# Attention and mixture of experts in one kernel: rows sent a tile earlier, VectorE's work regrouped, three shared blocks and paired row scatters between attention and experts

## The chip, the core and the metric

The kernel runs on one core of a Trainium2 chip. The metric is device time in microseconds (us), the median of several runs. The core's engines each take their instructions in order: PE (TensorE, matmuls), DVE (VectorE), ACT (ScalarE), POOL (GpSimd) and SP (SyncE, here for issuing transfers). They wait for each other through semaphores; transfers run on DMA engines. The xr and ys of the text are buffers in the device's memory.

## The reference

`x` has 4096 rows (tokens) of 256 numbers. Two sublayers are added to it in turn.

- Cross attention: `x = x + LayerNorm(q + Attention(q, ctx) Wo)` with `q = layernorm(x)`, 16 heads of 64, and 77 context rows for each of 4 batches. Per token and head there are 77 scores, a softmax, and a weighted sum of values.
- Mixture of experts: with `h = layernorm(x)`, each token's scores `softmax(h Wg)` over 32 experts pick its best 4. Each of these computes `silu(h W1[e]) * (h W3[e]) @ W2[e]` (256 to 128 to 256) times the score. An expert holds at most 4 x 4096 x 4 / 32 = 2048 pairs. Every token also passes a shared SwiGLU with inner width 256. Both are added to `x`.

All data are 32 bit floats. The 16384 pairs of token and expert must be sorted by expert before the experts' products can be made.

## The kernel before, in words

The 4096 rows are 32 tiles of 128 (`t`), four to a block (`blk`, 0 to 7; `c` is the tile in its block). The code calls block 6 `y` and block 7 `z`.

Attention is folded: prepared products `mq` hold keys times query weights, so that scores come straight from the normalised rows (`scores`, L418), in three groups of 6, 5 and 5 heads. For each group VectorE takes the maxima (L438), ScalarE the exponentials with their sums (`soften`, L441); then VectorE inverts the sums (`invert`, L454), POOL divides (`divide`, L458), PE transposes the probabilities (`turn_p`, L468), and multiplies them with values times output weights (`output`, L491). `residual` (L502) adds the rows. One tile of the loop issues the scores of tile t and the transposes and output of tile t-1.

Around that, the same loop carries the rest of each block in steps at fixed tiles. `measure_in`, `scale_in`, `norm_in`, `turn_in` and `bias_in` prepare the next block; `keep` (L400) adds a bias row to its rows. `measure_out` and `settle` (L508, L517) do the LayerNorm behind the attention, a tile each; `measure_ffn` and `norm_ffn` the one ahead of the experts. Two blocks behind come the experts' scores: `turn_ffn` (transposes pxn, L552), `gate` (lg, L566), `turn_gate`, `chances` and `powers` (softmax), `choose` (the best four, L596), `mark` (one-hot `oh` and `mask`, L619 and L626), `count` (prefix counts by matmul, pf, L638) and `place` (row numbers, L643). `send` (L669) then scatters one row of 128 pairs: POOL issues an indirect DMA which writes 128 rows of 1088 bytes from SBUF to their places in xr. There are 16 of them per block, 128 in all. From tile 11 on the loop sends four per tile, after the division.

When the loop has ended, blocks y and z still have to be sorted. This stretch is called the gap. In it stand, interleaved by hand: the rest of y's and z's steps, the shared SwiGLU of blocks y, 0 and z (`shared_in`, L696, product ph and activation sg; `shared_mid`, L716; `shared_out`, L724, product pz; `shared_add`, L739), and the tables. `tables` (L876) works out from the counts per expert which expert and which rows of xr each of the experts' tiles has: table "a" for tiles 0 to 63, which rest on blocks 0 to 5 alone, in four steps, and table "z" for the others. VectorE copies a table from PSUM at L938 to L941. The gap's scatters are issued in lots, `sends(3)`, `sends(2)`, `sends(7)`, `sends(12)` and `sends(20)`, with no wait between the scatters of a lot; the five transfers of expert weights (`load_experts`, L166) are issued first on SP, 3 MB in all.

The experts follow: 128 tiles of 128 rows in a fixed loop and 16 more in a second one. SP fetches eight tiles at a time (`fetch`, L1030), register loads giving the addresses; each is 136 KB. A tile goes through four steps, one per turn of the loop: transposes pgT (L1089), products peh with the tile's weights (L1097), ScalarE's activation h (L1105), and output py (L1118), which POOL scatters into ys (L1123). At the end every token's four results are gathered and added.

No scheduler moves this work. Inside `as_written` (L327), instructions of an engine keep the order in which the code issues them; only the row scatters that stand in an unbroken run on POOL, and likewise the results, may change places among themselves:

```python
kind = kinds.get(i.name)
before, run, of = runs.get(i.engine, ([], [], None))
if kind is None or kind != of:
    before, run = run, []
for name in before:
    tc.add_manual_dep(i, name, NOSYNC, reason="as written")
```

Of the kernel before, what the change touches and what calls it, by code (L numbers as in the profile page):

```python
# [9 lines left out]
F32 = mybir.dt.float32  # L10
# [20 lines left out]
def kernel(  # L31
# [73 lines left out]
    iota_j = const.tile([P, NJ], F32, name="iota_j")  # L105
    nc.gpsimd.iota(iota_j, [[1, NJ]], base=0, channel_multiplier=0, allow_small_or_imprecise_dtypes=True)
# [260 lines left out]
    def means(name):  # L367
        return sm.tile([P, NC, 2], F32, tag="mv", name=f"mv_{name}", bufs=6)
# [300 lines left out]
    def send(blk, i0, i1):  # L669

        row, xn = rows[blk], xns[blk]
        for i in range(i0, i1):
# [12 lines left out]
            if blk < BA:  # L685
                early.append(sct.ins)
            else:

                tc.declare_no_dep(sct.ins, group="firsts", reason="distinct rows")
                tc.add_to_no_dep_group("lates", sct.ins)  # L690

# [56 lines left out]
    measure_in(0)  # L748
    scale_in(0)
    norm_in(0)  # L750
    turn_in(0)
    bias_in(0)
    keep(0, 0, NC)
    xts[1] = load(1)
    with as_written():
        for t in range(NT):
            blk, c = t // NC, t % NC
            ffn, old = blk - 1, blk - 2
            ahead = blk + 1 < NB
            if c == 0 and blk + 2 < NB:  # L760
                xts[blk + 2] = load(blk + 2)
            if t == 0:

                nc.sync.dma_start(xr[NE * PLACES :, :], none)
                nc.sync.dma_start(
                    xr[: NE * PLACES, :].rearrange("(e q) r -> q e r", q=PLACES)[:P],
                    none.unsqueeze(1).to_broadcast([P, NE, ROW]),
                )
            if t == 18:
                nc.sync.dma_start(ws13[:, :, 0, :], Ws1.rearrange("(k p) f -> p k f", p=P))  # L770
                nc.sync.dma_start(ws13[:, :, 1, :], Ws3.rearrange("(k p) f -> p k f", p=P))
                nc.sync.dma_start(ws2, Ws2.rearrange("(k p) f -> p k f", p=P))
            if t in parts:
                load_experts(*parts[t])
            if c == 1 and ahead:
                scale_in(blk + 1)
            if c == 1 and ffn >= 0:
                measure_out(ffn, 2, 4)
            if c == 3 and ahead:
                bias_in(blk + 1)  # L780
            if c == 3:
                measure_out(blk, 0, 2)
            if c == 3 and ffn >= 0:
                measure_ffn(ffn)
            if c == 1 and old >= 0:
                gate(old)
            if c == 3 and old >= 0:
                count(old)
            sv = [scores(t, g) for g in range(2)]
            if c == 1 and old >= 0:  # L790
                turn_gate(old)
                chances(old)
            soften(t, 0, sv[0])
            if c == 1 and old >= 0:
                powers(old)
            soften(t, 1, sv[1])
            sv.append(scores(t, 2))
            if t >= 1:
                for i in range(3):
                    turn_p(t - 1, i)  # L800
            soften(t, 2, sv[2])
            if c == 0 and old >= 0:
                turn_ffn(old)
            if c == 2 and ahead:
                turn_in(blk + 1)
            if c == 0 and ahead:
                measure_in(blk + 1)
            if c == 1 and old >= 0:
                choose(old)
            if c == 2 and old >= 0:  # L810
                mark(old)
            if c == 3 and old >= 0:
                place(old)
            invert(t)
            divide(t)
            if c == 1 and ahead:
                norm_in(blk + 1)
            if c == 3 and ffn >= 0:
                norm_ffn(ffn)
            if c == 3:  # L820
                settle(blk, 0)
            elif ffn >= 0:
                settle(ffn, c + 1)
            if c >= 2 and ahead:
                keep(blk + 1, 2 * c - 4, 2 * c - 2)
            if t >= 11:
                b11, c11 = divmod(t - 11, NC)
                send(b11, c11 * TOPK, (c11 + 1) * TOPK)
            if t >= 1:
                residual(t - 1, output(t - 1))  # L830

        sxs[0] = late.tile([P, NC, D], F32, tag="qb", name="sx_0", bufs=3)
        sxs[0] = sxs[0].rearrange("p c d -> p (c d)").rearrange("p (k t) -> p k t", k=KC)
        nc.sync.dma_start(sxs[0], xnd[0])
        z, y = NB - 1, NB - 2
        assert BA == y
        msum_a = sm.tile([P, NE], F32, tag="msum_a", name="msum_a", bufs=1)
        nc.vector.tensor_copy(msum_a, cums[BA][:, 0, :])  # L840
        left = [(y - 1, i) for i in range(NK)]

        def sends(n):
            for blk, i in left[:n]:
                send(blk, i, i + 1)
            del left[:n]

# [5 lines left out]
        for i in range(3):  # L853
            turn_p(NT - 1, i)
# [465 lines left out]
```

## Time and profile before

| | us |
|---|---|
| median of three runs (lowest, highest) | 794.02 (792.67, 794.72) |
| time of the profiled execution | 795.5 |
| its span, first to last instruction | 793.7 |
| preparation | 0 to 61.8 |
| attention loop, 32 tiles, about 42.4 a block | 61.8 to 401.6 |
| gap | 401.6 to 482.6 |
| experts | 482.6 to 731 |
| gather, addition and store | 731 to 793.7 |

The mean TensorE clock granted over the span is 0.973. Stretches are cut by hand where one kind of work gives way to the next; the experts' first tiles overlap the end of the gap. To read the profile: an engine's idle time in front of an instruction is put down to the engine whose signal came last. Where no instruction is found whose end fits the signal, the trace names it "remote", or "another core or an unknown queue". Ends of matmuls are modelled. A run of equal instructions may be drawn as one line with a count.

### The profile page before, as it was taken

What the parts mean: (1) busy time and instruction counts of PE and PEld (TensorE: products, weight loads), DVE (VectorE), ACT (ScalarE), POOL (GpSimd) and SP (SyncE); (2) the same over time, 40 slices, a digit from 0 to 9 for tenths busy, and PEclk for the clock granted to TensorE, in tenths of its full rate; (3) what the DMA queues carried; (4) which work ended last, traced back from release to release, by engine and by line L of the source; (5) the groups of instructions that cost most, each with busy time, mean ns of one, the idle gap of its engine ahead of it and who ended that gap; (6) DMA issues with size and microseconds to landing.
All of it is one profiled execution on the core that took longest, in us unless ns stands there. A gap on an engine that the chain in (4) does not pass through costs nothing.

```text
span 793.7 us, 12911 instructions
## 1 busy us (share of the span) xinstructions
PE 726.8 (92%) x3508; PEld 540.2 (68%) x3508; DVE 526.8 (66%) x1455; ACT 334.3 (42%) x1586; POOL 403.3 (51%) x488
## 2 busy tenths in 40 slices
PE   6999999999999999999975569999999999999883
PEld 4775777677777777776743347888888878776452
DVE  1874565787778777776753336666667666564797
ACT  0647666766667776766621002222222222221100
POOL 2003333346878777786887354555555555534000
PEclk9999999999999999999999688999999999999997
DMA  8930000403226131514183523465655544522997
GB/s 270 331 107 1 1 0 2 124 10 114 79 72 213 58 130 57 155 51 142 57 243 107 159 94 110 143 209 178 210 159 170 166 158 143 175 89 74 404 396 282
DMA packets 78866, 111.96 MB, mean 141 GB/s; under 512 B 9995, under 2 KB 63679, under 8 KB 78783
## 3 DMA queue, kind: packets, MB, share of 16 engines
q1 hardware_dynamic: 59663, 66.66, 27.0%
q0 software_dynamic: 13056, 36.72, 12.8%
q10 hardware_dynamic: 6064, 7.64, 2.8%
q8 instruction: 31, 0.51, 0.3%
q14 instruction: 52, 0.43, 0.2%
HBM read 62.36 MB, written 48.64 MB: 140 GB/s over the span
## 4 chain that ended last, share of the span: by engine, by line
PE 66%; DVE 12%; ACT 6%; DMA 4%; another core or an unknown queue 4%; POOL 3%; issue 3%; SPq 0%; DVEq 0%; ACTq 0%; POOLq 0%
PE peh L1097 15%; PE po L497 14%; PE sc L430 13%; PE py L1118 7%; ACT p L446 5%; PE pgT L1089 4%; PE pp L479 2%; DVE gy L1213 2%; PE phT L1111 2%; PE ph L704 2%; DMA gy<-ys 2%; DVE y L1214 1%; POOL xr L674 1%; PE pvo L262 1%
## 5 line engine op out<-in xcount | busy, mean ns | idle before, releaser
L1123 POOL DMA_INDIRECT ys<-y,place x144 | 138.5, 962 | 120.7 <-DVE y L1122 81.0
L446 ACT ACTIVATE p<-sc,mx 128x77 f32<-128x77 f32 x512 | 159.5, 352 | 93.1 <-DVE mx L438 93.1
L1097 PE MATMUL peh<-we,gT 128*128 x576 | 151.9, 387 | 7.6 <-DVE gT L1091 7.1
L497 PE MATMUL po<-we,pT 128*128 128x256 f32 (+1 forms) x640 | 147.4, 384 | 4.6 <-DVE pT L484 3.3
L674 POOL DMA_INDIRECT xr<-xn,row x128 | 127.8, 999 | 46.5 <-issue 35.1
L461 POOL TENSOR_TENSOR p<-p,su 128x385 f32<-128x385 f32 (+1 forms) x96 | 91.1, 974 | 97.4 <-DVE su L456 76.5
L430 PE MATMUL sc<-we,qT 128*128 128x385 f32 (+1 forms) x384 | 138.9, 509 | 0.9 <-POOL qT L416 0.9
L497 PEld LDWEIGHTS po<-we,pT 128*128 128x128 f32 (+1 forms) x640 | 118.4, 190 | 27.1 <-DVE pT L484 5.4
L1105 ACT ACTIVATE h<-peh 128x128 f32<-128x128 f32 x144 | 40.0, 278 | 196.6 <-PE peh L1097 118.8
L446 ACT ACTIVATION_READ_ACCUMULATOR p<-sc,mx 128x1 f32 x512 | 119.4, 233 | 0.0
L1097 PEld LDWEIGHTS peh<-we,gT 128*128 128x128 f32 x576 | 99.9, 193 | 17.2 <-DVE gT L1091 8.4
L430 PEld LDWEIGHTS sc<-we,qT 128*128 128x128 f32 x384 | 71.1, 189 | 54.3 <-issue 27.6
L1106 DVE TENSOR_TENSOR h<-peh,h 128x128 f32<-128x128 f32 x144 | 42.0, 291 | 73.8 <-ACT h L1105 68.7
L1118 PE MATMUL py<-we,ehT 128*128 x288 | 86.6, 383 | 0.0
L1122 DVE TENSOR_SCALAR y<-py,own 128x256 f32<-128x256 f32 x144 | 69.6, 483 | 11.3 <-PE py L1118 10.3
L438 DVE TENSOR_REDUCE mx<-sc 128x5 f32<-128x385 f32 (+1 forms) x96 | 54.3, 576 | 33.2 <-PE sc L430 31.6
L1091 DVE COPY gT<-pgT 128x256 f32<-128x256 f32 x144 | 59.8, 415 | 6.7 <-PE pgT L1089 3.1
L1089 PE MATMUL pgT<-ident,g 128*128 128x128 f32 x288 | 55.6, 276 | 0.4 <-issue 0.4
L1118 PEld LDWEIGHTS py<-we,ehT 128*128 128x128 f32 x288 | 44.0, 193 | 11.9 <-issue 1.2
L1089 PEld LDWEIGHTS pgT<-ident,g 128*128 128x128 f32 x288 | 40.5, 143 | 15.1 <-issue 1.4
L730 PE MATMUL pz<-ws,hT 128*128 128x256 f32 x128 | 34.3, 419 | 15.3 <-DVE hT L719 14.4
L479 PEld LDWEIGHTS pp<-ident,p 128*128 128x128 f32 x320 | 36.1, 138 | 11.4 <-issue 5.5
(200 smaller groups left out, 933.6 us busy)
## 6 DMA issues: line engine op xcount, KB each, us to landing
g<-xr SPq DMA_DIRECT2D x144, 136.0 KB
gy<-ys SPq DMA_DIRECT2D x16, 1024.0 KB
xr<-y SPq DMA_DIRECT2D x1, 4352.0 KB
y<-in_x SPq DMA_DIRECT2D x8, 512.0 KB
out<-y ACTq DMA_DIRECT2D x16, 256.0 KB
xnd<-xnT SPq DMA_DIRECT2D x6, 512.0 KB
we<-in_W SPq DMA_DIRECT2D x8, 384.0 KB
ys<-y,place POOLq DMA_INDIRECT x144
```

The costliest lines, as they stand in the source:

```text
L430: nc.tensor.matmul(sc[:, : (h1 - h0) * SK], qTs[blk][:, k, o : o + P], mq[:, b, k, h0 * SK : h1 * SK], start=(k == 0), stop=(k == KC - 1),)
L438: nc.vector.tensor_reduce(mx[:, h0:h1], sv, AX.X, ALU.max, negate=True)
L446: nc.scalar.activation(probs[t][:, h, :], sv[:, h - h0, :], AF.Exp, bias=mx[:, h : h + 1], accum_out=su[:, h : h + 1],)
L461: nc.gpsimd.tensor_tensor(p[:, h0:h1, :], p[:, h0:h1, :], su[:, h0:h1].unsqueeze(2).to_broadcast([P, h1 - h0, SK]), ALU.mult,)
L497: nc.tensor.matmul(po[:, :D], pT[:n, i, :], vo[b][:n, i, :], start=(i == 0), stop=(i == KT - 1))
L674: sct = nc.gpsimd.indirect_dma_start(out=xr, out_offset=bass.IndirectOffsetOnAxis(ap=row[:, i : i + 1], axis=0), in_=xn[:, c, :], in_offse ...
L1089: nc.tensor.transpose(pt[:, k * P : (k + 1) * P], g[:, j % RG, k * P : (k + 1) * P], ident)
L1091: nc.vector.tensor_copy(gT.rearrange("p k t -> p (k t)"), pt[:, :D])
L1097: nc.tensor.matmul(ph[:, : 2 * H], gT[:, k, :], we[:, ds(ev[j] * EW + k * 2 * H, 2 * H)], start=(k == 0), stop=(k == KC - 1),)
L1118: nc.tensor.matmul(py[:, :D], hT, we[:, ds(ev[j] * EW + KC * 2 * H, D)], start=True, stop=True)
L1122: nc.vector.tensor_scalar(y, py[:, :D], own[:, i, 1:2], None, ALU.mult)
L1123: sent = nc.gpsimd.indirect_dma_start(out=ys, out_offset=bass.IndirectOffsetOnAxis(ap=place_[:, i : i + 1], axis=0), in_=y, in_offset=None,)
```

## The change

The loop: `mark` moves from tile c = 2 to c = 1, behind the division; `count` and `place` from c = 3 to c = 2; so that the sends begin at tile 10, four a tile and six at tile 31, from a list `left`. `keep` of a block moves from the block before (c = 2 and 3, two each) to its own c = 0, ahead of the reciprocal; the first block's `keep` moves from the preparation to tile 0. `settle` of the block before moves: tile 1 ahead of the reciprocal of c = 0, tile 2 behind its division, tile 3 ahead of the reciprocal of c = 2. `measure_in` moves from c = 0 to the c = 3 before it, and `measure_out` is split in halves for c = 0 and c = 1. In the last block, tiles 30 and 31, the normalisation, transposes and gate product of y are issued inside the loop, and the steps of table "a" too, whose wide temporaries share the buffer of `oh`; its expert numbers come from a product with `ones` in place of the helper column `e_col`.

The gap: the same three shared blocks, y, 0 and z. `sends` can make the first scatter of a lot wait for the last instruction issued. y's 16 scatters go out in eight lots of two, the first lot without such a wait; of z's 16, eight go out in the gap in twos and eight in the experts' loop, one every sixth tile. The fetches of the first sixteen experts' tiles are issued in the gap, on SP ahead of the five weight transfers, into a pool of their own.

The built order on POOL behind `place(y)`, where scatters may change places: seven scatters that wait for no such instruction, then one that waits for ScalarE's normalisation of z, two free ones, one that waits for z's transposed copy, and five that wait one after another for PE's pz of y, ScalarE's `powers`, its sg of block 0, VectorE's `shared_mid` and the copy of z's counts. Behind `place(z)`: two free ones, one waiting for sg of z, three free ones, and then one each for pz of block 0, the second sg of z, and pz of z.

The diff, with parts of the tables, of the old gap and of unchanged lines left out:

```diff
+            room = lt2.tile([P, NK, NE], F32, tag="oh", name="room").rearrange("p n e -> p (n e)")
+            oj, t1, t2, t3 = (room[:NE, i * NA : (i + 1) * NA] for i in range(4))
...
-    keep(0, 0, NC)
...
+    z, y = NB - 1, NB - 2
+    assert BA == y
+    left = []
+    def sends(n, after=None):
+        for i, (blk, k) in enumerate(left[:n]):
+            sct = send(blk, k, k + 1)
+            if after is not None and i == 0:
+                tc.add_manual_dep(sct, after, SYNC, reason="rows in small lots")
+        del left[:n]
+    def last():
+        return nc.cur_bb.bb.instructions[-1].name
...
-            if c == 1 and ffn >= 0:
-                measure_out(ffn, 2, 4)
+            if c < 2 and ffn >= 0:
+                measure_out(ffn, 2 + c, 3 + c)
             if c == 3 and ahead:
                 bias_in(blk + 1)
             if c == 3:
                 measure_out(blk, 0, 2)
-            if c == 3 and ffn >= 0:
+            if c == 3 and ffn >= 0 and not end:
...
-            if c == 3 and old >= 0:
-                count(old)
...
+            if c == 2 and old >= 0:
+                count(old)
...
+            if c == 3 and end:
+                turn_ffn(y)
...
+            if c == 3 and end:
+                gate(y)
+                next(ta)
...
-            if c == 0 and ahead:
-                measure_in(blk + 1)
+            if c == 0:
+                keep(blk, 0, NC)
+                if ffn >= 0:
+                    settle(ffn, 1)
             if c == 1 and old >= 0:
                 choose(old)
             if c == 2 and old >= 0:
-                mark(old)
-            if c == 3 and old >= 0:
                 place(old)
+                left += [(old, i) for i in range(NK)]
+            if c == 2 and ffn >= 0:
+                settle(ffn, 3)
+            if c == 3 and blk + 2 < NB:
+                measure_in(blk + 2)
+            if t == 0:
+                measure_in(1)
+            if c == 3 and end:
+                settle(z, 0)
+                next(ta)
...
+            if c == 0 and ffn >= 0:
+                settle(ffn, 2)
...
-            if c == 3 and ffn >= 0:
+            if c == 1 and old >= 0:
+                mark(old)
+            if c == 2 and end:
+                measure_ffn(y)
+            if c == 3 - end and ffn >= 0:
                 norm_ffn(ffn)
-            if c == 3:
+            if c == 3 and not end:
                 settle(blk, 0)
-            elif ffn >= 0:
-                settle(ffn, c + 1)
-            if c >= 2 and ahead:
-                keep(blk + 1, 2 * c - 4, 2 * c - 2)
-            if t >= 11:
-                b11, c11 = divmod(t - 11, NC)
-                send(b11, c11 * TOPK, (c11 + 1) * TOPK)
+            sends(6 if t == NT - 1 else TOPK)
             if t >= 1:
                 residual(t - 1, output(t - 1))
+            if t == NT - 2:
+                ta = tables("a", cums[BA][:, 0, :], NA)
+                next(ta)
...
+        turn_gate(y)
+        next(ta)
+        chances(y)
+        powers(y)
         for i in range(3):
             turn_p(NT - 1, i)
-        settle(z, 2)
-        residual(NT - 1, output(NT - 1))
+        sends(3)
+        choose(y)
+        settle(z, 1)
+        mark(y)
+        po = output(NT - 1)
+        count(y)
+        sends(3, last())
+        assert not left
+        residual(NT - 1, po)
         measure_out(z, 3, 4)
-        gate(y)
-        turn_gate(y)
-        chances(y)
-        powers(y)
-        settle(z, 3)
-        sends(2)
-        measure_ffn(z)
+        place(y)
+        left += [(y, i) for i in range(NK)]
...
+    with as_written():
+        shared_in(y, 0, AF.Tanh)
+        settle(z, 2)
+        settle(z, 3)
+        measure_ffn(z)
+        sends(2)
+        shared_in(y, 1, AF.Tanh)
+        shared_mid(y, 0)
+        norm_ffn(z)
+        sends(2, last())
+        fetch(0)
+        fetch(RG)
+        for part in range(5):
+            load_experts(*parts[NT + 1 + part])
+        shared_mid(y, 1)
+        turn_ffn(z)
+        sends(2, last())
+        shared_out(y)
+        sends(2, last())
+        gate(z)
+        turn_gate(z)
+        chances(z)
+        powers(z)
+        sends(2, last())
+        shared_in(0, 0, AF.Silu)
+        sends(2, last())
+        choose(z)
+        mark(z)
+        shared_mid(0, 0)
+        sends(2, last())
+        shared_in(0, 1, AF.Silu)
+        count(z)
+        msum_z = sm.tile([P, NE], F32, tag="msum_z", name="msum_z", bufs=1)
+        nc.vector.tensor_copy(msum_z, cums[NB][:, 0, :])
+        tz = tables("z", msum_z, NJ - NA)
+        sends(2, last())
+        place(z)
+        assert not left
+        left += [(z, i) for i in range(NK)]
+        shared_mid(0, 1)
+        shared_in(z, 0, AF.Silu)
+        sends(2, last())
+        shared_out(0)
+        sends(2, last())
+        shared_mid(z, 0)
+        shared_add(y)
+        shared_in(z, 1, AF.Silu)
+        sends(2, last())
+        shared_mid(z, 1)
+        shared_add(0)
+        shared_out(z)
+        sends(2, last())
+        shared_add(z)
...
-        fetch(0)
         for j in range(NM_ + len(steps)):
-            if j % RG == 1 and j + RG - 1 <= NM_:
+            if j % RG == 1 and RG < j + RG - 1 <= NM_:
...
+            if j % 6 == 0:
+                sends(1)
```

## The prediction

> **What bounds the kernel now.** I read the page's busy shares and forty slices first, to find where TensorE rests.
>
> ```profile
> PE 726.8 (92%) x3508; PEld 540.2 (68%) x3508; DVE 526.8 (66%) x1455; ACT 334.3 (42%) x1586; POOL 403.3 (51%) x488
> PE   6999999999999999999975569999999999999883
> POOL 2003333346878777786887354555555555534000
> PEclk9999999999999999999999688999999999999997
> ```
>
> PE is the bound except in the slices from about 400 to 480 us, where the clock falls too. The windows cut there (start:end, length, then busy us of PE, PEld, DVE, ACT and POOL, then clock, DMA share, GB/s):
>
> ```profile
> 186.00:228.00 42.00, 41.69 (x205) 30.63 (x203) 32.63 (x90) 29.27 (x154) 32.53 (x41) 1.00 0.29 97
> 401.60:445.70 44.10, 23.01 (x104) 11.66 (x103) 19.00 (x81) 7.79 (x15) 30.69 (x38) 0.85 0.50 161
> 462.80:482.60 19.80, 12.95 (x46) 9.04 (x43) 6.28 (x24) 2.23 (x9) 8.42 (x9) 0.74 0.17 63
> 482.60:580.00 97.40, 95.91 (x532) 80.36 (x532) 67.98 (x220) 24.76 (x115) 55.38 (x59) 1.00 0.55 176
> ```
>
> A block of four attention tiles leaves PE 0.3 us idle, the experts 1.5 in 97. The gap wastes 21 + 7. The chain of waits says on what (start, us, what):
>
> ```profile
> 425.50 17.95 another core or an unknown queue
> 444.62 1.03 DVE mask L626
> 445.69 1.48 PE pf L638 x4
> ...
> 457.80 15.71 another core or an unknown queue
> ```
>
> The timelines show what stood there (start, us, instruction, idle before it):
>
> ```profile
> 425.04 0.27 PE L934 MATMUL p_r_a<-t_a,ones 32*1 32x64 f32 x2
> 443.43 0.21 DVE L938 TENSOR_SCALAR r_tab_a<-p_r_a 1x64 int32<-1x64 f32 x1 [17.93 <-remote]
> 445.69 0.79 PE L638 MATMUL pf<-mask,tri 128*128 128x128 f32 x2 [16.40 <-DVE mask L626]
> 473.53 0.28 ACT L1105 ACTIVATE h<-peh 128x128 f32<-128x128 f32 x1 [15.73 <-remote]
> 410.23 1.57 POOL L674 DMA_INDIRECT xr<-xn,row  x1 [0.19 <-issue]
> 439.43 0.96 POOL L674 DMA_INDIRECT xr<-xn,row  x1 [0.30 <-issue]
> 470.60 0.96 POOL L674 DMA_INDIRECT xr<-xn,row  x1 [0.31 <-issue]
> ```
>
> VectorE's table copy L938 needs only PE's product p_r_a, done at 425.3, yet starts at 443.43. The trace's record of PE's signals has none between 422.10 and 443.40, and then four in 0.16 us. Likewise h (L1105) starts at 473.53, long after peh. Both releases come about 3 us after POOL's last row scatter of an unbroken run: 24 scatters at 1.27 us from 410.23 to 440.4, 15 from 452.85 to 471.6. Signals of the first run begin to lag after four scatters (2.1 us at 414.3), of the second after eight. Loop tiles issue four and show no hold; expert results 1.63 us apart show none. So I read: while scatters run back to back, PE's signals are held. The trace doesn't show by what.
>
> **The change, part by part.** T counts from the scores of tile 31 (382.97 before). Before: the last output ends at T 18.7, experts begin at 79.9 (462.86). Their tiles, 1.63 us apart, count back to a start of 93.6, as 476.6 is tile 9's 491.23 less 9 periods: first matmul at T 83.3, then slow ramp, half clock and 1.7 us for the late gathers of tile 8.
>
> *Loop.* Marking, counting, placing and sending one tile earlier, measure_out in halves, keep and settle at new places: same instructions. PE has 0.3 us of idle per block, so the gain is 0 (at most 7 x 0.3 = 2). Their cover is the stretch to the next reciprocal: after the tile's maxima VectorE waits 4.2 us for the exponentials. With c = 0 it now gets four keeps (4 x 0.43 to 0.68) and settle 1 (0.43 + 0.48 to 1.06) plus half a measure_out (0.6): 3.2 to 4.8. An overrun of 0.6 first eats the 3 us between divide and transposes; if that cover were gone, 0.6 x 7 = 4. I take 0. POOL has 32.5 busy of 42 in a block and sends as many rows per tile, so its queue is no fuller. Only tile 0 shows a late reciprocal: keep(0) leaves the preparation and joins measure_in(1) there. It ended 68.9 and the reciprocal ran at 69.34; 4 x 0.43 more make it 70.6: +1.3, in full, since nothing stands behind.
>
> [...] In the rows settle's last step takes 0.48 alone and 1.06 under a divide, so moving two settles and four keeps off the divides saves VectorE 2 x 0.58 + 4 x 0.25 = 2.2 us per block. [...]
>
> *Tiles 30 and 31.* Gate of block y (6) and table a move in. PE then waits for the normalised block (about 1.6) and its gate chain (1.6), less half a microsecond of the waits that stand there now; output 31 ends near T 21.4 instead of 18.7. In return the gate's product and three of four table steps are over by then.
>
> *The gap.* PE was busy 56.6 of the 79.9 us from the scores of 31 to the experts; 2.1 of it is the low clock of the third window (0.88 of 17.2), so its work is 54.5 at full clock. To it come the 3.2 above. Added: prefix counts of y wait for its mask, 2.7 (chances, powers, choose, mark: from T 15 to 24); the transposes of z wait for its norm, 3.5 without a hold. 54.5 + 3.2 + 2.7 + 3.5 = 63.9. From the first transposes to the first peh it was 3.4 before; I take 4 with its ramp: start 67.9. Removed: the hold on the table, since L938's product is now made in tiles 30 and 31, behind which are no more than six scatters.
>
> *Scatters in twos.* As many as before. The first of a pair waits for the instruction last written, but row scatters may move among themselves and the built order on POOL uses it: after place(y) seven stand in a row without such a wait, then waits come one by one with up to four free ones between. Queued behind each wait are the other scatters and VectorE's place of z through POOL's copies; fetches on SP wait for the landed rows. Bounds: no hold at all, 0; both holds in full, 16.4 + 15.7. [...] By the rows, seven in a row (9 us) are more than the four after which lag began, and less than 24. I take 6 us on y's run and 3 to 5 on z's, 10 in all, with ramp.
>
> *Fetches and weights.* Sixteen gathers (0.53 us each) now stand on SP ahead of five weight loads. First gather when the earlier rows have landed, T 34; sixteen issued by 45, weights by 51. They took 14 us to land before, so T 57 to 65; first use 65 to 74. Hidden, margin near zero at worst. Gathers of tile 8 come early: 1.7 saved. Eight scatters of z go into the experts, one per six tiles: 9 of POOL's idle 40% there; hidden.
>
> *Sum.* Start before 93.6. After, 67.9 + 10 = 77.9, plus 1.3 for tile 0 and 2 for a remaining dip of the clock: 81.2. Gain 12.4. Against the profiled execution, whose span is 793.7 and its whole time 795.5, 783.1; that execution stood 1.5 above the median of the runs, 794.0, so 781.6. I say 782.
>
> **Rivals.** *A, likeliest, 0.42:* holds shrink but remain, 782, own range 776 to 790. *B, holds gone, 0.19:* for it, loop scatters in fours and spaced results show none; against it, the seven in a row. 93.6 - 67.9 - 1.3 = 24.4; with a dip, 795.5 - 24.4 + 2 - 1.5 = 772. *C, the gain is used up, 0.12:* the change doesn't do what it says, because the free scatters run as one train again and one hold of 15 stays on the path: 67.9 + 15.7 + 1.3 + 5 of clock and late weights = 89.9; 795.5 - 3.7 - 1.5 = 790, or, with the loop's overrun of 4, 794. *D, slower, 0.27:* both holds return in full, one on POOL's train behind place(y), one behind place(z), and now stall residual, z's mask and the ramp: 67.9 + 16.4 + 15.7 + 1.3 = 101.3, 7.7 beyond 93.6: 802. It decides once the holds on the path pass 93.6 - 69.2 = 24.4 us. For it: 24 of the 32 scatters of y and z are still in the gap, and seven free ones follow y's place; against it: the waits break the train, and the table's copy no longer lies under it.
>
> **How the numbers follow.** About 0.3%, 2.4 us, is what a measurement of this kernel can tell from no change. A gives 0.39 faster and 0.03 within; B 0.19 faster; C 0.04 faster, 0.06 within, 0.02 slower; D 0.02 within, 0.25 slower: faster 0.62, within 0.11, slower 0.27. The range leaves out one in ten at each end: from half of B's mass, 769, to most of D's, 802.
>
> **What would show it.** Right: no stretch without a PE signal over 6 us; table a's copy within 1 us of its product; first expert transposes near T 74; weights landed before the first peh; loop blocks at 42.0 to 42.5; tile 0's reciprocal at 70.6. Wrong: "remote" waits of 15 us after place(y) or place(z); a peh waiting for its weights; PE idle over 1 us a block before the transposes.

## The result

The changed kernel takes 800.34 us (median of 7, 797.56 to 804.14) beside 794.02 of the kernel before (792.67 to 795.5): ratio 1.0084, 95% interval 1.0059 to 1.0109. It is slower by 0.6% to 1.1%. The profiled execution has a span of 798.6 us, 4.9 more than before.

The page of the changed kernel:

```profile
PE 733.0 (92%) x3508; PEld 541.3 (68%) x3508; DVE 524.1 (66%) x1457; ACT 334.3 (42%) x1586; POOL 401.8 (50%) x501
PE   6998999999999999999994898998999999999883
POOL 2003343357777778777667355656555555534000
PEclk9999999999999999999997799999999999999997
```

PE's hole around 420 us is smaller than before, but two of the four slices between 480 and 560 us have fallen from nines to eights. The windows, cut at the new borders (start:end, length, busy us of PE, PEld, DVE, ACT, POOL, then clock, DMA share, GB/s):

```profile
186.00:228.00 42.00, 41.04 (x202) 30.17 (x201) 31.71 (x88) 29.57 (x154) 31.87 (x42) 1.00 0.29 94
387.40:412.90 25.50, 22.92 (x107) 16.24 (x107) 16.46 (x64) 10.20 (x46) 16.48 (x20) 0.87 0.15 50
412.90:467.20 54.30, 38.75 (x129) 22.25 (x129) 20.97 (x59) 8.68 (x15) 32.95 (x43) 0.84 0.56 176
481.40:588.10 106.70, 97.43 (x514) 77.41 (x513) 65.99 (x214) 24.96 (x112) 60.29 (x63) 1.00 0.53 168
```

A stretch of the loop now has 0.96 us of PE idle, which was 0.31. Tile 31 takes 25.4 us from its scores to its output, which was 18.7, and its granted clock is 0.87. The gap behind it has 15.6 us of idle, and the tiles 8 to 64 of the experts 9.3 in 106.7.

Laid over each other by the starts of the same matmuls, the two traces give a ledger whose parts add up to the spans. The experts' first tiles overlap the gap, so the start of steady experts is reckoned back from tile 8: its first product, less eight periods of 1.627 us. "Start" below always means this, counted from the scores of tile 31.

| stretch | before | after | difference |
|---|---|---|---|
| to the scores of tile 31 | 382.97 | 387.43 | +4.46 |
| from there to the start of steady experts | 91.96 | 81.00 | -10.96 |
| the eight periods | 13.02 | 13.02 | 0 |
| experts, tiles 8 to 64 | 94.26 | 106.69 | +12.43 |
| tile 64 to the end | 211.47 | 210.42 | -1.05 |
| sum | 793.68 | 798.56 | +4.88 |

So the gap did become shorter, by about what was forecast. What it won was lost again by the experts, and the loop's loss came on top.

The chain of waits of the changed kernel shows the remote waits that are left (start, us, what):

```profile
429.59 13.05 another core or an unknown queue
...
514.81 4.09 another core or an unknown queue
...
542.05 4.11 another core or an unknown queue
```

There is one of 13 us in the gap, and new ones of 4 us stand where experts run. Timelines from there, of POOL and of ScalarE:

```profile
511.71 0.96 POOL L1154 DMA_INDIRECT ys<-y,place  x1 [1.96 <-DVE y L1153]
512.97 0.96 POOL L1154 DMA_INDIRECT ys<-y,place  x1 [0.30 <-DVE gT L1122]
514.29 0.96 POOL L1154 DMA_INDIRECT ys<-y,place  x1 [0.36 <-issue]
515.55 0.96 POOL L672 DMA_INDIRECT xr<-xn,row  x1 [0.30 <-issue]
516.81 0.96 POOL L1154 DMA_INDIRECT ys<-y,place  x1 [0.30 <-issue]
```

```profile
518.90 0.28 ACT L1136 ACTIVATE h<-peh 128x128 f32<-128x128 f32 x1 [3.85 <-remote]
```

One scatter of z's rows (L672) among the results makes five in a row, 1.26 to 1.32 us apart. ScalarE waits 3.85 us for PE's signal (1.2 to 1.5 in the tiles just before) and gets it about 1 us after the row has ended; four signals of PE then come within 0.15 us. The results that were late follow each other closely too, so the next short row needs no extra scatter: from 520.16 on three start 1.26 and 1.40 us apart. Tiles longer than 1.8 us go on until tile 55.

### The profile page after: what moved, and what is told of

The parts are those of the page before. It is cut to its first block, busy times and chain, and to the rows that moved or that the text cites. A ratio compares the mean times of both kernels' runs of the same rounds, so it can differ in the third digit from the quotient of the medians.

```text
span 798.6 us, 12943 instructions
## 1 busy us (share of the span) xinstructions
PE 733.0 (92%) x3508; PEld 541.3 (68%) x3508; DVE 524.1 (66%) x1457; ACT 334.3 (42%) x1586; POOL 401.8 (50%) x501
## 4 chain that ended last, share of the span: by engine, by line
PE 71%; DVE 9%; DMA 6%; POOL 4%; issue 3%; another core or an unknown queue 3%; ACT 3%; SPq 1%; DVEq 0%; ACTq 0%; POOLq 0%
PE po L495 16%; PE peh L1128 14%; PE sc L428 14%; PE py L1149 7%; PE pgT L1120 4%; PE ph L703 3%; PE pp L477 2%; DVE gy L1245 2%; PE phT L1142 2%; POOL xr L672 2%; DMA y<-in_x 2%; DMA gy<-ys 1%; ACT p L444 1%; POOL p L459 1%
## 5 line engine op out<-in xcount | busy, mean ns | idle before, releaser
L1128 PE MATMUL peh<-we,gT 128*128 x576 | 149.9, 383 | 8.6 <-DVE gT L1122 4.5
L495 PE MATMUL po<-we,pT 128*128 128x256 f32 (+1 forms) x640 | 150.5, 390 | 6.5 <-DVE pT L482 3.1
L672 POOL DMA_INDIRECT xr<-xn,row x128 | 127.4, 995 | 47.2 <-issue 38.2
L428 PE MATMUL sc<-we,qT 128*128 128x385 f32 (+1 forms) x384 | 141.3, 513 | 0.9 <-POOL qT L414 0.9
L495 PEld LDWEIGHTS po<-we,pT 128*128 128x128 f32 (+1 forms) x640 | 121.0, 194 | 29.8 <-issue 8.1
L459 POOL TENSOR_TENSOR p<-p,su 128x385 f32<-128x385 f32 (+1 forms) x96 | 85.7, 919 | 103.9 <-DVE su L454 79.3
L1128 PEld LDWEIGHTS peh<-we,gT 128*128 128x128 f32 x576 | 98.3, 190 | 19.6 <-DVE gT L1122 6.3
```

Source lines behind the costliest of these rows:

```text
L428: nc.tensor.matmul(sc[:, : (h1 - h0) * SK], qTs[blk][:, k, o : o + P], mq[:, b, k, h0 * SK : h1 * SK], start=(k == 0), stop=(k == KC - 1),)
L459: nc.gpsimd.tensor_tensor(p[:, h0:h1, :], p[:, h0:h1, :], su[:, h0:h1].unsqueeze(2).to_broadcast([P, h1 - h0, SK]), ALU.mult,)
L495: nc.tensor.matmul(po[:, :D], pT[:n, i, :], vo[b][:n, i, :], start=(i == 0), stop=(i == KT - 1))
L672: sct = nc.gpsimd.indirect_dma_start(out=xr, out_offset=bass.IndirectOffsetOnAxis(ap=row[:, i : i + 1], axis=0), in_=xn[:, c, :], in_offse ...
L1128: nc.tensor.matmul(ph[:, : 2 * H], gT[:, k, :], we[:, ds(ev[j] * EW + k * 2 * H, 2 * H)], start=(k == 0), stop=(k == KC - 1),)
```

## The experiments

Runs that stand beside the kernel before share its chip. Not all chips behave alike, and no number here can be read without that: on that of the result and on two of the experiments' chips the kernel before takes 793 to 795 us, on three others 766 to 767. The first are called chips with holds, the others chips without. A hold is a stretch in which PE's signals reach the engines that wait for them only microseconds after the matmul has ended; so the table's copy in the kernel before waited for 17.9 us.

### z's scatters out of the experts' loop

```diff
-        sends(2, last())
+        sends(10, last())
+        assert not left
         shared_add(z)
...
-            if j % 6 == 0:
-                sends(1)
```

> The changed kernel, with all sixteen scatters of block z issued in the gap (ten in the last lot) and none in the experts' loop. Theory S (signals of PE are held while POOL issues scatters back to back; the eight late ones fill POOL's rests and so start trains in the experts): from tile 16 to tile 64 of the experts it takes 78 us as before the change, not 89.4; but a train of sixteen stands over the experts' ramp and holds the first activation by 5 to 10 us. Total 792 to 799 against 800.3. Rival R (the experts are slowed by the earlier fetches and their own pool, not by the late scatters): the stretch from tile 16 to 64 stays near 89, total 800 to 808.

Measured on a chip with holds: 800.53 beside 793.21, ratio 1.0096 (1.0064 to 1.0128). Tiles 16 to 64 take 78.36 us, as in the kernel before, and not 89.38. The start moves from 81.0 to 90.9, with a row of 15 scatters over the experts' first tiles; the first activations wait up to 4.7 us for remote signals there. The late eight cost the experts 11, and in the gap they cost 10. The rival, that the earlier fetches slow the experts, is refuted: they are unchanged here. The total is above the expected 792 to 799.

### The late eight alone, in the kernel before

```diff
-        sends(20)
-        assert not left
+        sends(12)
+        assert len(left) == 8
...
+            if j % 6 == 0:
+                sends(1)
```

> The kernel before, with only one part of the change: the last eight scatters of block z leave the gap and go out in the experts' loop, one every sixth tile. Theory S: the stretch from tile 16 to 64 rises from 78.4 to 86 to 90 us, the hold on the first activation (15.7 us) shrinks to under 6 since its train has seven instead of fifteen; total 790 to 800. Rival R: the stretch stays at 78 to 79, total 784 to 788.

Measured: 794.25 beside 793.21, ratio 1.0016 (1.0006 to 1.0025). Tiles 16 to 64 take 87.62 against 78.36; the start comes at 81.1 against 92.0. One part of the change, alone, shows both halves of the ledger. On a second chip with holds it came out the same, 795.93 beside 794.7, ratio 1.0015 (1.0001 to 1.0028), with 90.1 us for tiles 16 to 64:

> The kernel before with z's last eight scatters in the experts' loop, every sixth tile, again: on the chip with holds it took 1.0 more than the kernel before (12 us won in the gap, 9 lost among the experts, and a little at the end). Theory P for a chip without holds: POOL, scattering without a pause, bounds the gap's end there (its queue reaches the first results 10 us late, and tiles 9 to 11 lose 8 us in all); eight fewer cost nothing later, so 758 to 762 against 766. If PE bounds the gap there, 765 to 767.

The expectation for a chip without holds could not be tried, since this run came to one with them. Twelve late scatters instead of eight, on the same chip:

> As before_late_eight, with z's last twelve, every fourth tile. Theory P for a chip without holds: no further gain once POOL is no longer behind, so within 1.5 us of before_late_eight_2, since an extra scatter per four tiles (1.27 us) still fits the 0.36 us that each tile of 1.63 leaves POOL. On a chip with holds: 16 to 64 takes over 90 us, total 2 to 6 above before_late_eight_2.

```diff
-        sends(12)
+        sends(8)
...
-            if j % 6 == 0:
+            if j % 4 == 0:
```

800.64 beside 794.7, ratio 1.0088 (1.0062 to 1.0114). Tiles 16 to 64 take 93.0, and the start comes at 77.1: more is won in the gap and more lost behind it.

### True pairs

```diff
-            if after is not None and i == 0:
+            if after is not None:
```

> The changed kernel, with the second scatter of each lot waiting for the same instruction as the first, so that at most four stand free in a row in the gap. Theory S: the hold on the copy of z's gate scores (13 us, 9 us of PE idle) falls under 3 us and the total by 6 to 9, to 791 to 795; the experts' stretch from 16 to 64 stays near 89. Rival Q (what counts is how many scatters are under way since the loop's end, not how densely they stand): the hold stays over 8 us, total 798 to 802.

Measured on a chip with holds: 794.09 beside 793.21, ratio 1.0008 (0.9995 to 1.0021). The number of scatters is the same, and the longest row in the gap falls from 12 to 8. The windows of the same stretch, first of the changed kernel and then of this one:

```profile
401.00:470.00 69.00, 51.63 (x186) 32.20 (x185) 33.12 (x106) 9.88 (x20) 42.34 (x52) 0.85 0.48 153
```

```profile
401.00:470.00 69.00, 57.55 (x231) 37.47 (x230) 39.18 (x130) 12.26 (x30) 45.91 (x56) 0.93 0.49 159
```

PE does 6 us more work in it, at a higher clock, and no remote wait is left in the gap. The experts' stretch stays at 89.4, as expected, since the late eight are still there. That speaks for the density of the scatters and against their number. The edit takes away what the change lost: here it can't be told from the kernel before.

### The one-hot ahead of the reciprocal

```diff
             if c == 1 and old >= 0:
                 choose(old)
+                mark(old)
...
-            if c == 1 and old >= 0:
-                mark(old)
```

> The changed kernel, with the one-hot and mask of a block made ahead of the reciprocal of its tile c = 1 (behind the choice of the best four) and not behind its division. Theory L (there it delays the residual and the first maxima of the next tile by 1.3 us, and with them the exponentials and ScalarE's copies that the output products wait for): blocks from the fourth on take 42.4 us again, not 43.3; with six such blocks 4 to 5 us off, total 795 to 797. Rival: the reciprocal is 2 us later and eats the rest ahead of the transposes, blocks stay at 43 or rise; total 800 to 805.

VectorE's timeline of the changed kernel, at the border between c = 1 and c = 2 of a block:

```profile
331.89 0.25 DVE L454 RECIPROCAL su<-su 128x16 f32<-128x16 f32 x1 [0.61 <-ACT p L444]
...
332.79 1.07 DVE L624 TENSOR_REDUCE mask<-oh 128x128 f32<-128x512 f32 x1
333.89 1.76 DVE L628 TENSOR_TENSOR cum<-cum,mask 128x32 f32<-128x32 f32 x4
335.57 0.42 DVE L503 TENSOR_TENSOR qb<-po,qb 128x256 f32<-128x256 f32 x1
...
336.58 0.60 DVE L436 TENSOR_REDUCE mx<-sc 128x6 f32<-128x462 f32 x1
```

The tile's scores begin at 333.50, and their first maxima 3.1 us later. Before it was 1.8 (330.18 and 332.00). The one-hot, mask and sums stand in front of the residual, and the residual in front of the maxima. Under the division (2.83 us from 332.32 on) the four sums take 1.76 us; ahead of the reciprocal, in the kernel before, 0.87. Why they are slower there, no trace shows. PE feels the delay at the output products: it stands 0.54 us before them at 340.8, and with the edit not at all.

Measured on a chip with holds: 797.19, ratio 1.0062 (1.0037 to 1.0087). The total's interval overlaps that of the changed kernel, so the loop is read from the trace: from the scores of tile 4 to those of tile 28 it takes 254.24 us, 256.73 with the change and 253.47 before. Three quarters of the loop's loss lie in this step; from the fourth block on 0.3 to 0.7 us per block remain, now between the scores of c = 0 and those of c = 1.

### The root of y's normalisation ahead of the division

```diff
+            if c == 2 and end:
+                measure_ffn(y)
             if c == 3 and blk + 2 < NB:
...
-            if c == 2 and end:
-                measure_ffn(y)
```

> The changed kernel, with the reciprocal root for block y's normalisation (POOL's ve and rs) issued ahead of the division of tile 30 and not behind it. Theory N (in tile 31 VectorE stands 4.2 us before sh, which waits for rs behind that division, with the residual and the maxima of tile 31 queued behind it): that wait falls under 1, and output 31 ends 3 to 4 us earlier against the scores of tile 31 (now 25.4 behind their start, 18.7 in the kernel before); total 795.5 to 797.5 against 800.3. Rival: PE's transposes, gate and ScalarE's copies of y set the end of tile 31 anyway, so output 31 moves by less than 1.5, total 799 to 801.

`measure_ffn` makes the reciprocal root of the variance (POOL's ve and rs), which VectorE needs for the shift sh. VectorE in the changed kernel:

```profile
386.27 0.25 DVE L454 RECIPROCAL su<-su 128x16 f32<-128x16 f32 x1 [0.28 <-ACT p L444]
390.69 0.16 DVE L359 SCALAR_TENSOR_TENSOR sh<-mv,rs 128x4 f32<-128x4 f32 x1 [4.17 <-POOL rs L348]
...
392.35 1.08 DVE L436 TENSOR_REDUCE mx<-sc 128x6 f32<-128x462 f32 x2
```

and with the root ahead of the division:

```profile
387.82 0.92 DVE L359 SCALAR_TENSOR_TENSOR sh<-mv,rs 128x4 f32<-128x4 f32 x1 [0.96 <-POOL rs L348]
...
390.24 1.23 DVE L436 TENSOR_REDUCE mx<-sc 128x6 f32<-128x462 f32 x2
```

This run's chip had no holds: 775.7 beside 766.63, ratio 1.0105 (1.0056 to 1.0154), so the number in the expectation can't be compared, but the stretch can. From the scores of tile 31 to its output it takes 20.88 us; the changed kernel takes 23.34 on a chip without holds, and the kernel before 18.7. VectorE's wait fell from 4.2 (on both kinds of chip) to 1.0. On the chip with holds the changed kernel took 25.44: in that trace 6.8 us of the tile lie at half clock (granted clock 0.87 over the tile), and in the one without holds none (1.00). So the root is worth 2.5 us, and the other 2.1 go with the clock.

### Both kernels on a chip without holds

> The kernel before, unchanged, for its trace on this call's chip. Two chips have run so far: on one it took 793.2 us and the changed kernel's variants showed held signals, with a third of PE's signals missing from the records; on the other it took 766.6, variants showed no hold and every signal was recorded. Theory S' (the holds under dense scatters belong to the chip): on a chip of the first kind the trace has holds of 16 to 18 us in the gap and a stretch from experts' tile 16 to 64 of 78.4; on one of the second kind no wait for a remote signal over 2 us, experts begin 28 us earlier, total 765 to 768. Rival T (the difference lies in the rate of transfers or the clock everywhere): the loop or the tail differs by over 5 us.

> The changed kernel, unchanged, beside it. On a chip of the first kind 799 to 801, a hold of 13 us in the gap and 89 us from tile 16 to 64. On one of the second kind theory S' expects none of both: 78.4 us from tile 16 to 64, the losses of the loop (4) and of tiles 30 and 31 (6 to 7) left, of which the gap gives nothing back: 776 to 780 against 766.

Measured: the kernel before 767.28, against 765.92 for its shared runs; the changed one 778.51, ratio 1.0159 (1.0113 to 1.0205). The page of the kernel before on this chip:

```profile
PE   6999999999999999999998997999999999999882
PEclk9899999999999999999999999999999999999998
```

The hole is gone, and nearly all of the clock's fall in the gap with it (1.00 granted from 401.6 to 455 us). POOL scatters there without a pause, 49 in a row from 412.6 to 475.1 us, at most 1.63 apart and most of them 1.26, and no engine waits over 0.5 us for a remote signal. The trace then has a record of every signal that PE gives (1228 for 1227 matmuls that signal); in the changed kernel's trace on this chip each record stands at most 0.05 us behind the end of its matmul.

On chips with holds 824 to 937 of PE's signals are recorded. In the kernel before the missing ones begin near 180 us, where the loop's scatters begin, and end with the last result. They are not PE's alone: 1041 of VectorE's 1304 are recorded, 523 of ScalarE's 682, and 4404 landings of transfers where the other chip has 8167. The lag is PE's alone: in the changed kernel's trace 48 of PE's records stand over 0.5 us behind the last end ahead of them, and of VectorE's, ScalarE's and POOL's none over 0.02.

Loop and tail take the same time on both kinds of chip, within 0.3 us, which refutes the rival. The ledger here, from one trace to the other: +3.70 to the scores of tile 31, +8.42 from there to the start (60.73 to 69.15), -2.38 for tiles 8 to 64, -0.31 for the rest, +9.43 in all.

### Three edits together

The last three diffs (true pairs, the one-hot, the root) on the changed kernel.

> Three edits together on the changed kernel: both scatters of a lot wait, the one-hot ahead of the reciprocal, rs of y ahead of the division. If the three losses stand in different stages and are independent, the gains add: 6.2 (measured) + 3.1 (measured) + 3 to 4 for the third: 787 to 789. If the earlier start only meets another wait at the experts' ramp (fetches, weights), 790 to 794.

The second of these runs also had

```diff
-            if j % 6 == 0:
+            if j in (0, 1, 2, 10, 20, 30, 40, 50):
                 sends(1)
```

> As three_mended, with the eight late scatters of z in the experts' tiles 0, 1, 2, 10, 20, 30, 40 and 50 instead of every sixth: three of them stand where no result is scattered yet. Theory S: each extra scatter among the results starts a train that costs 1 to 1.5 us; with five instead of seven such the stretch from tile 16 to 64 falls from 88 to 84 to 86, total 2 to 4 us below three_mended. If the loss there depends on anything but those scatters, no difference within 1 us.

> The changed kernel with both scatters of a lot waiting, the one-hot ahead of the reciprocal and rs of y ahead of the division, again beside both kernels. On a chip of the first kind the gains should add: 786 to 790 against 793. On one of the second kind it took 773.7.

> The changed kernel with both scatters of a lot waiting, the one-hot ahead of the reciprocal and rs of y ahead of the division, beside the others. On a chip where the kernel before takes 793 the three gains should add, 786 to 790; on one where it takes 766, 773 to 774.

All four runs came to chips without holds: 773.68, 773.88, 773.21 and 774.0, ratios 1.0084, 1.0089, 1.0082 and 1.0093 to the kernel before, each interval within 1.006 to 1.0124. Against the 1.0159 of the changed kernel the edits win back about half. Where the late scatters stand makes no difference there (tiles 16 to 64 take 78.4 to 78.6), so without holds they are hidden. Whether the edits add up on a chip with holds was not seen.

### The queue on POOL behind the loop

On a chip without holds PE still waited 6.2 us for z's transposes. VectorE and POOL of the three edits together:

```profile
417.93 0.54 DVE L524 SCALAR_TENSOR_TENSOR y<-qb,rs,y 128x256 f32<-128x256 f32 x1 [5.22 <-POOL rs L513]
```

```profile
409.35 1.09 POOL L672 DMA_INDIRECT xr<-xn,row  x1 [0.19 <-issue]
...
416.00 0.96 POOL L672 DMA_INDIRECT xr<-xn,row  x1 [0.30 <-issue]
416.99 0.25 POOL L510 TENSOR_SCALAR ve<-mv 128x1 f32<-128x1 f32 x1
417.32 0.58 POOL L513 TENSOR_TENSOR rs<-ve,neg_half 128x1 f32<-128x1 f32 x1
```

A root of 0.58 us stands behind six scatters. It was put ahead of them, and then the next root too:

```diff
-        sends(3)
...
-        sends(3, last())
-        assert not left
         residual(NT - 1, po)
         measure_out(z, 3, 4)
+        sends(6)
+        assert not left
```

> As three_mended, and behind the loop POOL makes the reciprocal root of z's last tile (measure_out of tile 3) before it issues the last six scatters of block 5 and not behind them. Theory Z (on a chip without holds PE stands 6.2 us before z's transposes, because VectorE's settle of z's last tile waits 5.2 us for that root behind six scatters): the wait for the root falls under 1, that of PE to 1 to 2.5, and the experts begin 4 to 5 us earlier; 3.5 to 5 us below three_mended. Rival: the normalisation waits for other work of VectorE (place and mask of y) in its stead, gain under 1.5.

Without holds: 772.45, ratio 1.0058 (1.0026 to 1.0089), 1.5 below the three edits on the same chip and not 3.5 to 5. VectorE's wait for that root is gone, but sh then waits 4.1 us for the root of the normalisation, behind the same six, and PE's wait falls only from 6.2 to 5.1. With both roots ahead:

```diff
-        sends(6)
-        assert not left
...
         measure_ffn(z)
-        sends(2)
+        sends(8)
```

> As rs_first, and the root of z's normalisation too is made on POOL ahead of block 5's last six scatters. In rs_first the stall only moved: the next root stood behind the same six (4.1 us), gain 1.1. Theory Z: with neither behind them PE's wait for z's transposes falls from 5.1 to about 1 us and the experts begin 4 us earlier than in rs_first; on a chip without holds 768 to 770 against 766. Rival: z's rows then wait for VectorE or the table loads, gain under 1.5.

This one ran on a chip with holds: 798.48 beside 794.7, ratio 1.0058 (1.0028 to 1.0087). PE's first wait for z's rows is 1.1 us, as expected. But 22 scatters now stand in a row, a remote wait of 17.0 us is back, and another resource has moved. PE's and SP's timelines:

```profile
467.32 1.10 PE L1124 MATMUL peh<-we,gT 128*128 x4 [4.15 <-DMA we<-in_W]
```

```profile
426.82 24.90 SPq L1001 DMA_DIRECT2D g<-xr  x16
451.76 5.23 SPq L169 DMA_DIRECT2D we<-in_W  x4
```

The gathers wait for block 5's rows, which are sent later, and the weights stand behind the gathers on SP: they land 4 us after they are needed.

### Scatters spaced by other work

```diff
                 send(blk, i, i + 1)
+                nc.gpsimd.tensor_tensor(filler, ones[:, 0:1], neg_half[:, 1:2], ALU.pow)
```

> The kernel before, with a small power of one column (0.58 us where the trace has that form) on POOL behind each of the gap's scatters: the same scatters in the same order, only no longer back to back, 1.9 us apart instead of 1.27. Theory S (what holds PE's signals is the density of the scatters): the holds of 17.9 us ahead of the table's copy and of 15.7 ahead of the first activation fall under 4 each, although POOL ends its scatters some 20 us later; total 778 to 790, the end of the scatters at the ramp limiting the gain. Rival Q (the number of scatters, or their landing in memory, holds the signals): the holds last as long as POOL's run, so they get longer, total 795 to 815.

> The kernel before with a power of one column on POOL behind each scatter of the gap, again. On a chip of the second kind it took 791.4, since POOL comes to its first result 25 us late. On one of the first kind theory S expects both holds under 4 us, but the same late POOL: 788 to 795; rival Q (it is their number): holds as before or longer, 800 to 815.

> The kernel before with POOL's small power behind each scatter of the gap. On a chip where the kernel before takes 793: theory S (density) expects no wait for a remote signal over 4 us in the gap, rival Q (number) holds of 16 us or more; the total is 790 to 796 by S, since POOL's lateness costs 25 us anyway, and over 805 by Q. Where the kernel before takes 766: 791 to 795, as before.

All three came to chips without holds: 791.41, 794.54 and 794.5, ratios 1.0321 to 1.0366. The question of density they could not answer. They price POOL instead: it comes to the results late, and tiles 8 to 16 take 43 to 45 us instead of 20.9. In the kernel before, without holds, these tiles already lose 7.9 us (20.9 against 13.0), since POOL has no pause there and VectorE waits 3.8 us for a buffer of results; the change's moved scatters win 2.7 of them. No version tried is faster than the kernel before on either kind of chip.

### Rows of scatters and holds

On chips with holds, by the traces of the gap, each row being scatters less than 1.75 us apart, and waits over 2 us:

| kernel | row | longest remote wait in it |
|---|---|---|
| before | 22, then 15 | 20.8 (17.9 for the table's copy), then 15.7 |
| changed | 12, then 8 | 13.1, then none |
| z's sixteen in the gap | 12, then 15 | 12.9, then 4.7 |
| one-hot early | 12, then 8 | 12.9, then none |
| true pairs | at most 8 | none |
| before with late eight, two chips | 22, then 8 | 21.7 and 21.9, then none and 3.4 |
| before with late twelve | 15 | 10.2 |
| both roots first | 22, then 6 | 17.0, then none |

The length of a row alone doesn't give the wait: two rows of 15 over the experts' first tiles gave 15.7 and 4.7. Nor is eight a safe number. True pairs still has lags up to 1.9 us behind its row of eight, which no engine in the gap feels as a long wait. Among the experts' results, where each tile takes 1.63 us, five in a row gave waits of 3.9.

## Why the prediction was wrong

Forecast were 781.6 and measured 800.3, 18.7 more. The ledger splits this: 12.4 among the experts' tiles 8 to 64, 3.2 in the loop (4.5 instead of 1.3), 2.7 in the gap (11.0 won, not 13.7), less 1.1 behind tile 64, and 1.4 because the profiled execution stood 1.5 above the median before and at the median after.

**"Eight scatters of z go into the experts ... hidden" is the step that failed.** It counted POOL's time, 9 us in an idle 40%, and put the hold there at nothing. As POOL's time the term was right: on a chip without holds tiles 16 to 64 take 78.6 us with the late eight and 78.2 without. But on chips with holds it is rows that count. With the 0.30 us between two scatters a tile of 1.63 leaves POOL only 0.36, so one extra scatter (1.27) uses up the rests of three tiles and makes a row. Tiles 8 to 64 took 12.4 us more; with that term alone the forecast of 782 becomes 794, no gain. Taking the eight out gave 11.0 us back between tiles 16 and 64; adding them to the kernel before cost 9.3 there. The prediction had the reading in hand, "the four after which lag began", and did not apply it to the stage where a scatter every 1.63 us left least room.

**The gap came out near, in part by luck.** The sum put the start of the experts from 93.6 to 77.9 plus 2 for the clock, a gain of 13.7. Measured were 91.96 and 81.00 (the 93.6 was reckoned back from tile 9, which gives 1.6 more). Its terms missed in both directions. Too small were the output of tile 31 (by 4.0), the hold on y's row (6 us of PE idle, measured 9.1) and the wait for z's transposes (3.5, measured 6.0). Too large were the hold on z's row of eight (3 to 5, measured none) and the wait of y's prefix counts for the mask (2.7, measured none). The two long waits of PE:

```profile
426.17 2.80 PE L550 MATMUL pxn<-ident,xn 128*128 128x128 f32 x8 [5.97 <-ACT xn L363]
442.99 0.48 PE L579 MATMUL lt<-ident,pr 128*128 128x128 f32 x1 [9.12 <-ACT pr L577]
```

The second is y's hold: PE waits for ScalarE's copy of z's gate scores (pr), which itself waits 13.1 us for a remote signal. True pairs, which take this hold away, bring the start to 72.5. That the holds come with dense rows was the right reading of the profile. Its counts were a little off: the first run has 23 scatters, not 24, and the first late signal (2.1 us at 414.3) stands behind three of them. What one chip's trace could not show is that other chips have no holds.

**"I take 0" for the loop was wrong in its place.** It looked at tile c = 0 and its room ahead of the reciprocal. Most of the loss is behind the reciprocal of c = 1: the one-hot after that division pushes the next tile's maxima by 1.3 us. From the scores of tile 4 to those of tile 28 this and smaller shifts cost 3.3, and a block takes 43.3 us instead of 42.4. The 1.3 us for `keep` in tile 0 were too much: the first reciprocal comes 0.8 later behind the first scores (8.4 and 7.6). Up to the scores of tile 4 the loop lost 2.5 in all. The other 1.7 go with the clock: from 72.2 to 75.6 us this trace has half clock (granted clock 0.5), and the changed kernel's trace on a chip without holds, which has full clock there, lost 0.8. The preparation, without `keep`, was 1.5 shorter.

**Tiles 30 and 31 were mis-sized.** Predicted was an output at 21.4 instead of 18.7, measured 25.4. Left out was POOL's queue: y's root waits for a division, VectorE stands 4.2 us for it, and the maxima of tile 31 are queued behind. On a chip without holds, at full clock, the output comes at 23.3, and with the root ahead of the division at 20.9, near the forecast.

**The transposes of z** waited 6.0 instead of 3.5 for a similar reason: a root behind six scatters. With both roots ahead PE waited 1.1.

**Fetches and weights** were right: the weights were no wait in the changed kernel. The margin, near zero at worst, was real; both roots first overdrew it by 4.2 us. Of the 1.7 us for the gathers of tile 8 nothing came: tile 9 starts 3.9 us after tile 8, which was 3.3.

**The rivals.** A, the likeliest, named its mechanism rightly for the gap, but its range of 776 to 790 was missed. The slower case, 802, had nearly the right size for the wrong reason: it wanted both holds back in full around the placements, and there was one of 13 us. Holds did decide it, but among the experts. On a chip without holds the change is slower still, by 1.6%, because then only its losses remain; that case was not among the rivals.

What stays open: why some chips hold PE's signals under dense scatters. The spacing of scatters by other work, meant to part density from number, met only chips without holds. Another rival was not tried: every time on record comes with a span and a clock of the same execution, so none is known to be free of the recording, and records are missing just on the chips and in the stretches that have the holds. Whether the holds would be there without it, no run shows.

## What to carry to other kernels

A helper engine's share of busy time (POOL's was 55.38 of 97.40 us among the experts) doesn't tell whether more work fits on it. On the chips with holds what counted was how many of its scatters stood back to back: a single extra one, in a stream that leaves 0.36 us to spare in each tile, made a row. Before moving an operation, list what stands ahead of it on the helper engine's queue: three of the losses here were a root of 0.6 to 1.1 us behind a division or six scatters. And measure a change on more than one chip before reading its mechanism from one trace.

## What was not expected of the hardware

The kernel before took 766 to 767 us on three chips and 793 to 795 on the others. The loop from tile 4 to 28 takes the same (253.2 and 253.5), and so does the end from tile 127 (106.6 and 106.4). The difference lies in the gap: the start comes at 60.7 on a chip without holds and at 92.0 on one with them, where PE's signals come late while POOL scatters back to back and the clock falls (0.85 from 401.6 to 445.7 us); the tiles behind it give 4.8 back. With holds, rows of 12 to 22 gave remote waits of 4.7 to 22 us; without, 49 in a row gave none over 0.5. On the chips with holds a quarter to a third of PE's signals are missing from the records (824 of 1227 are there in the kernel before), and records of the other engines and of landings too. Missing records were thus a sign of the kind of chip in all twenty traces, which the profile of the kernel before already carried.
